# Attention and a mixture of experts on one core: small VectorE work moved or put in closed form, inputs loaded earlier, transfers issued a piece later

## The chip, the cores and the metric

The kernel runs on one core of one Trainium2 chip. The metric is the device time of one execution in microseconds. Five engines work from five queues of their own: TensorE (PE; the loading of its weights is shown apart as PEld), VectorE (DVE), ScalarE (ACT), GpSimd (POOL) and SyncE (SP), which here only issues transfers. [...]

## The reference

```python
# x: 8 sequences of 1024 tokens, 256 wide; 16 heads of 16; keys and values are one projection
x = x + attention(layernorm(x))          # softmax(q k^T / 4) k, then Wout and bout
y = layernorm(x)
x = x + moe(y)

def moe(x):                              # 8192 tokens
    scores = softmax(x @ gate_w.T)       # 8 experts
    vals, idx = top_k(scores.T, 1024)    # each expert takes its 1024 best tokens
    z = layernorm(x[idx]) * ln_w + ln_b
    out = gelu(z @ fc1.T + b1) @ fc2.T + b2
    return x.at[idx].add(out * vals)     # its own residual is inside
```

Every token passes three normalisations: before the attention (called a in the code), before the experts (b), and the expert's own (c), which normalises what b has already normalised.

## The kernel before

The first part is the attention with all that belongs to a token: projections, rotation, softmax, output projection, the second norm, the router. It runs over 8 batches (sequences) of 4 groups of heads; a group has 4 heads and takes 16 steps. A step handles one block of 128 keys for 512 queries (a half): scores for four heads, their exponentials, and in every second step the products with the values (`weigh_values`, L472). Step `s` counts from -15 to 512, so a batch has 64 steps, and batch b begins at step 64b.

The softmax needs the maximum of each query first. Row maxima are computed 15 steps ahead (`LEAD`): four matmuls in each step (L374), and after each a reduction of 512 scores on VectorE (L381). After each half of a group `lay_max` joins the two halves of the keys (L389), splits the result into a high and a low part (L391, L392), transposes both on TensorE (L398), and sends them through memory into `top_bufs` (L406, L410). They are added to the scores by a matmul eight steps after the half's last maximum.

The order on every engine is what the program writes; nothing is reordered. Beside the steps run three lists of tasks, written as generators: `urgent` (`lay_max`, and `divide`, which ends a half of a group), `starts` (the `prologue` of a later batch) and `ends` (the `epilogue` of each half of an earlier batch). A task says at each `yield` what it waits for: a number is a number of steps, "s" is at once, "y" needs a light step, "x" a heavy slot, of which each odd step has one. `run_pieces` (L622) goes through urgent, starts and ends in this order after each step, and of starts and ends it runs only the first task. A heavy slot goes to starts before ends.

The prologue of a batch loads x in two halves (L259), normalises them (L164 to L175), transposes (L184), projects (L303), rotates on GpSimd (L203 to L210), and splits queries, keys and the differences of keys (called steps) into high and low parts (`split_halves`, `split_steps`). `write_halves` (L216) writes these to memory, where `load_keys`, `load_steps` and `load_queries` fetch them for each group; `ready` and `steps_ready` say what has been written. High and low parts have two buffers each.

The epilogue fetches the residual (`residual`, L524) and adds the bias (L527), transposes and projects the attention's output (L548), adds (L556), takes the statistics for b (L164, L165, then two small GpSimd instructions L167, L169), scales the rows on GpSimd (`scaled`, L175), writes x plus y to the output (L562), takes statistics again for c and scales into `rows`, transposes (L184), and computes the router: a matmul (L579), a transpose (L590), and a small softmax (L593 to L605). In the last batch the scaling runs on VectorE. The value accumulators are added on GpSimd (L487).

Two places in the loop can run a task to its end at once. One is the start of a batch:

```python
if s > 0 and g == 0 and step == 0:
    while ends and ends[0].batch < b - 1:
        finish([ends[0]])
        ends.pop(0)
```

`finish` advances the task without a regard for slots, and the step's own matmuls come behind it. The other finishes the prologue when the keys or steps of a group are not there yet.

The second part finds each expert's tokens by 30 rounds of counting (L779 on), then gathers, computes and scatters (L860 on). The change does not touch it.

Of the kernel before, what the change touches and what calls it, by code (L numbers as in the profile page):

```python
# [18 lines left out]
P = 128  # L19
# [7 lines left out]
def preln_attention_moe_kernel(  # L27
# [50 lines left out]
    with ExitStack() as actx:  # L78
# [92 lines left out]

        def scaled(eng, dst, src, stats):
            mv, rstd = stats
            for t in range(T2):
                eng.tensor_scalar(  # L175
                    dst[:, t, :], src[:, t, :], mv[:, t, 0:1], rstd[:, t : t + 1],
                    ALU.subtract, ALU.mult,
                )
# [32 lines left out]

        def write_halves(d, rows, cols, hi, lo, keys):

            for part, src_t in enumerate((hi, lo)):
                pair = slice(part, None, 2) if keys else slice(2 * part, 2 * part + 2)
                nc.sync.dma_start(  # L216
                    d[rows, pair, cols], src_t.bitcast(F32).unsqueeze(1).to_broadcast([P, 2, QW])
                )

        def split_halves(b, hf, c, s, pt):  # L220

            q_d, k_d, _ = halves[b]
            first = b == 0 and c == 0
            hi = side.tile([P, QW], F32R, tag="hi", name="hi")
            lo = side.tile([P, QW], F32R, tag="lo", name="lo")
            full = None
            if first:
                nc.scalar.copy(hi, pt)
                nc.vector.tensor_tensor(lo, pt, hi.bitcast(F32), ALU.subtract)
            if not first or s == 1:  # L230
                full = side.tile([P, QW], F32, tag="full", name="full")
                nc.scalar.copy(full, pt)
            if not first:
                nc.gpsimd.tensor_copy(hi, full)
                nc.gpsimd.tensor_tensor(lo, full, hi.bitcast(F32), ALU.subtract)
            rows = slice(c * P, (c + 1) * P)
            if s == 0:
                write_halves(q_d[hf], rows, slice(0, QW), hi, lo, False)
            else:
                write_halves(k_d, rows, slice(hf * QW, (hf + 1) * QW), hi, lo, True)  # L240
            return full

        def split_steps(b, hf, c, full):


            dif = side.tile([P, QW], F32, tag="u", name="dif")
            nc.gpsimd.tensor_copy(dif[:, 0:P], full[:, 0:P])
            nc.gpsimd.tensor_tensor(dif[:, P:QW], full[:, P:QW], full[:, 0 : QW - P], ALU.subtract)
            hi = side.tile([P, QW], F32R, tag="hi", name="dhi")
            lo = side.tile([P, QW], F32R, tag="lo", name="dlo")  # L250
            nc.gpsimd.tensor_copy(hi, dif)
            nc.gpsimd.tensor_tensor(lo, dif, hi.bitcast(F32), ALU.subtract)
            write_halves(
                halves[b][2], slice(c * P, (c + 1) * P), slice(hf * QW, (hf + 1) * QW), hi, lo, True
            )
# [8 lines left out]
        def prologue(b):  # L264
# [7 lines left out]
            else:  # L272
                xts = [load_x(b, hf) for hf in range(2)]
                yield 2
# [36 lines left out]
            for c in range(DC):  # L311
                fulls = []
                for hf in range(2):
                    for s in range(2):
                        yield "x"
                        pt = transposed(lambda j: qks[hf][:, j, s, c * P : (c + 1) * P])
                        full = split_halves(b, hf, c, s, pt)
                    if hf == 1:
                        ready[(b, c)] = True
                    if b > 0 or c > 0:  # L320
                        yield 2
                        split_steps(b, hf, c, full)
                        yield 2
# [5 lines left out]
                steps_ready[(b, c)] = True  # L329
# [55 lines left out]
        def lay_max(i, hf):  # L385
# [3 lines left out]
            nc.vector.tensor_tensor(both, nm[:, 0], nm[:, 1], ALU.min)  # L389
            parts = small.tile([P, 4, 2, T2], F32R, tag="parts", name="parts")  # L390
            nc.vector.tensor_copy(parts[:, :, 0, :], both)  # L391
            nc.vector.tensor_tensor(  # L392
                parts[:, :, 1, :], both, parts[:, :, 0, :].bitcast(F32), ALU.subtract
            )
            yield 2
            yield "y"
# [7 lines left out]
            nc.scalar.copy(rows, pt[0 : 8 * T2, 0:P])  # L404
            top_d = dram.tile([2, 2, 2, QW], F32, tag="top_d", name="top_d", bufs=2)
            nc.sync.dma_start(  # L406
                top_d.rearrange("a h s (t q) -> (a h s t) q", q=P), rows
            )
            for h in range(2):
# [108 lines left out]
        def residual(b, hf):  # L518

            if (b, hf) not in residuals:  # L520
# [6 lines left out]
                nc.gpsimd.tensor_tensor(xt, xt, bo.unsqueeze(1).to_broadcast([P, T2, D]), ALU.add)  # L527
                residuals[(b, hf)] = xt
            return residuals[(b, hf)]

        def epilogue(b, hf):
# [4 lines left out]
            xt = residual(b, hf)  # L536
            yield "x"
# [23 lines left out]
            nc.gpsimd.tensor_tensor(xt, xt, xf, ALU.add)  # L561
            nc.sync.dma_start(out[b, tok, :].rearrange("(t p) d -> p t d", p=P), xt)  # L562
            yield 2

            rows = side.tile([P, T2, ROW], F32, tag="rows", name=f"rows_{b}_{hf}")
            if not last:
                stats = yield from row_stats(xf, "c")
                scaled(eng, rows[:, :, 0:D], xf, stats)
# [39 lines left out]
            if last:  # L608
                stats = yield from row_stats(xf, "c")
                scaled(eng, rows[:, :, 0:D], xf, stats)  # L610
# [56 lines left out]
        for s in range(-LEAD, n_steps + 1):  # L667
# [6 lines left out]
            if with_max and mstep == 0 and mi not in grp or with_exp and "steps" not in grp[i]:  # L674
                finish(starts)
                run_loads(s)
            if s == 0 or s > 0 and g == NG - 1 and step == T:
# [29 lines left out]
            if s == n_steps - 16:  # L707
                for hf in range(2):
                    residual(B - 1, hf)
# [318 lines left out]
```

## Time and profile before

| | |
|---|---|
| median of 3 runs | 2466.57 us (2464.75 to 2474.08) |
| profiled execution, its own time | 2478.25 us |
| its span, first to last instruction | 2476.5 us |
| score loop with its lead, about | 55 to 1800 us |
| TensorE busy | 87% |
| VectorE busy | 70% of the span; 85% from 500 to 1700 us |
| ScalarE, GpSimd busy | 55%, 51% |
| mean granted TensorE clock | 0.936 |

The profile is of one execution. Busy time counts an engine's instructions and not the waiting between them. In a row of a group, the two numbers after the bar are the time in which the group was busy and the mean length of one instruction in nanoseconds; the next is the time that the engine stood idle just before them, with what ended most of it. In the timeline, a row begins with the start and the length in microseconds, and a bracket gives the idle time before it and who ended it. PEclk is the clock that TensorE was granted, in tenths. A wait put down to one engine can have been for another, where the engine named was long done.

### The profile page before, as it was taken

How to read it: one execution, taken by the hardware profiler on the slowest of the kernel's cores; microseconds unless marked ns; L12 is line 12 of the kernel's file. 1: busy time of each engine (PE TensorE's matmuls, PEld its weight loads, DVE VectorE, ACT ScalarE, POOL GpSimd, SP SyncE). 2: the span in 40 equal slices, each digit the busy share in tenths (PEclk: the TensorE clock that was granted, in tenths of full speed). 3: DMA queues.
4: the chain of work that ended last, by engine and by line, in shares of the span. 5: the costliest groups of instructions: out<-in, count | busy, mean ns of one | idle time of the engine just before them, and what ended most of it. 6: DMA issues, size and time to landing. Idle time of an engine off the chain costs nothing. (4 is left out here: it accounts for less than half of the span.)

```text
span 2476.5 us, 34944 instructions
## 1 busy us (share of the span) xinstructions
PE 2149.9 (87%) x12692; PEld 1141.8 (46%) x12692; DVE 1740.0 (70%) x3303; ACT 1361.8 (55%) x1725; POOL 1253.4 (51%) x1188
## 2 busy tenths in 40 slices
PE   4999999988989989998998898999842189999998
PEld 2444444444544444444444344444321156666665
DVE  4988888887888888888888788999446833331111
ACT  1378777766777767776777676777820011111111
POOL 3365475648467665665674576544220144443332
PEclk7699999999999999999999999999965589999999
DMA  5514613532561453254235325331030023333322
GB/s 174 209 53 155 223 61 117 210 104 73 197 204 62 155 178 98 104 181 155 87 129 206 104 78 180 138 120 63 28 120 0 3 50 71 69 71 72 81 39 28
DMA packets 153564, 275.44 MB, mean 111 GB/s; under 512 B 14640, under 2 KB 66736, under 8 KB 153264
## 3 DMA queue, kind: packets, MB, share of 16 engines
q1 hardware_dynamic: 139984, 254.56, 29.7%
q0 software_dynamic: 12288, 17.05, 4.1%
q8 instruction: 100, 1.64, 0.3%
q10 hardware_dynamic: 1120, 1.61, 0.2%
q14 instruction: 72, 0.59, 0.1%
HBM read 146.02 MB, written 127.14 MB: 110 GB/s over the span
## 5 line engine op out<-in xcount | busy, mean ns | idle before, releaser
L381 DVE TENSOR_REDUCE nm<-ps_x 128x1 f32<-128x512 f32 x2048 | 1263.7, 681 | 211.7 <-PE ps_x L374 209.2
L453 ACT ACTIVATE e<-ps_s 128x1024 f32<-128x1024 f32 x1024 | 999.7, 1025 | 132.0 <-PE ps_x L374 77.0
L374 PE MATMUL ps_x<-k,q 64*128 64x512 f32 x2048 | 753.4, 460 | 41.3 <-DMA q<-q_d 17.3
L420 PE MATMUL ps_s<-q,s 64*128 64x512 f32 x2048 | 640.7, 430 | 9.3 <-ACT e L453 8.2
L374 PEld LDWEIGHTS ps_x<-k,q 64*128 64x128 f32 x2048 | 359.7, 190 | 450.7 <-DVE nm L381 295.1
L472 PE MATMUL ps_av<-e,v 128*32 128x512 f32 x4096 | 508.9, 616 | 42.6 <-DVE nm L381 39.2
L487 POOL TENSOR_TENSOR av<-av,avp 128x512 f32<-128x512 f32 x191 | 243.6, 1275 | 407.9 <-ACT avp L485 402.0
L420 PEld LDWEIGHTS ps_s<-q,s 64*128 64x128 f32 x2048 | 319.2, 187 | 42.6 <-ACT e L453 25.4
L939 ACT ACTIVATE hT<-ps_h,b 128x512 f32<-128x512 f32 x128 | 87.8, 687 | 369.5 <-PE ps_h L932 364.4
L954 DVE TENSOR_TENSOR o<-ps_o,b2b 128x256 f32<-128x256 f32 x64 | 27.2, 425 | 357.0 <-PE ps_o L946 357.0
L956 POOL DMA_INDIRECT out<-o,idx x64 | 127.2, 1988 | 281.8 <-DMA out<-o,idx 132.2
L472 PEld LDWEIGHTS ps_av<-e,v 128*32 128x32 f32 x4096 | 109.1, 111 | 292.8 <-issue 167.9
L932 PE MATMUL ps_h<-yT,w 128*128 128x512 f32 x512 | 225.8, 599 | 7.4 <-DVE yT L920 7.3
L946 PE MATMUL ps_o<-w,hT 128*128 128x256 f32 x1024 | 223.6, 379 | 0.0
L485 ACT COPY avp<-ps_av 128x512 f32<-128x512 f32 x192 | 112.6, 587 | 190.6 <-PE ps_av L472 179.4
L946 PEld LDWEIGHTS ps_o<-w,hT 128*128 128x128 f32 x1024 | 194.6, 190 | 33.3 <-issue 7.7
L420 PE MATMUL ps_s<-top,ones_r 64*128 64x512 f32 x512 | 151.7, 400 | 10.8 <-DMA top<-top_d 10.8
L932 PEld LDWEIGHTS ps_h<-yT,w 128*128 128x128 f32 x512 | 96.7, 191 | 125.0 <-issue 109.1
L904 POOL DMA_INDIRECT g<-rows_d,idx x64 | 70.5, 1102 | 147.4 <-DVE ids L879 128.2
L303 PE MATMUL ps_p<-wqkv,xnT 128*128 128x512 f32 x256 | 130.1, 636 | 15.4 <-DVE nm L381 15.0
L203 POOL TENSOR_TENSOR u<-pe,sin 128x256 f32<-128x256 f32 x112 | 79.1, 727 | 60.7 <-ACT pe L197 60.7
L420 PEld LDWEIGHTS ps_s<-top,ones_r 64*128 64x128 f32 x512 | 89.4, 189 | 20.6 <-DMA top<-top_d 12.1
(141 smaller groups left out, 1986.8 us busy)
## 6 DMA issues: line engine op xcount, KB each, us to landing
k<-k_d SPq DMA_DIRECT2D x64, 512.0 KB
q<-q_d SPq DMA_DIRECT2D x128, 256.0 KB
s<-s_d SPq DMA_DIRECT2D x64, 512.0 KB
q_d<-hi SPq DMA_DIRECT2D x32, 512.0 KB
q_d<-lo SPq DMA_DIRECT2D x32, 512.0 KB
k_d<-hi SPq DMA_DIRECT2D x32, 512.0 KB
k_d<-lo SPq DMA_DIRECT2D x32, 512.0 KB
s_d<-dhi SPq DMA_DIRECT2D x32, 512.0 KB
```

Of the source, the lines that this page charges most:

```text
L303: nc.tensor.matmul(pp, lhsT=xnT[:, c, j * P : (j + 1) * P], rhs=wqkv[:, c].rearrange("p a d -> p (a d)"), start=(c == 0), stop=(c == DC - 1),)
L374: nc.tensor.matmul(pt, lhsT=q[r : r + 64, h // 2, j * P : (j + 1) * P], rhs=k[r : r + 64, h // 2, kh * QW : (kh + 1) * QW], start=True, st ...
L381: nc.vector.tensor_reduce(grp[i]["nm"][:, kh, h, j : j + 1], pt, AX.X, ALU.max, negate=True)
L420: nc.tensor.matmul(pt[:, h % 2, :], lhsT=ones_r[r : r + 64, :] if last else k[r : r + 64, pair, kt * P : (kt + 1) * P], rhs=(top_bufs[half ...
L453: nc.scalar.activation(e.rearrange("p h q -> p (h q)"), pt.rearrange("p h q -> p (h q)"), AF.Exp, scale=DH**-0.5,)
L472: nc.tensor.matmul(pa[HS * h : HS * (h + 1), :], lhsT=v_bufs[b % 2][:, kt, c : c + HS], rhs=es[h // 2][:, h % 2, :], start=(n == 0), stop= ...
L485: nc.scalar.copy(part, pa)
L487: (nc.vector if end else nc.gpsimd).tensor_tensor(av, av, part, ALU.add)
L932: nc.tensor.matmul(ph, lhsT=w1[:, c, f * P : (f + 1) * P], rhs=yT[:, c, :], start=(c == 0), stop=(c == DC - 1),)
L939: nc.scalar.activation(hT[:, f, :], ph, AF.Gelu_apprx_tanh, bias=b1[:, e * FC + f : e * FC + f + 1])
L946: nc.tensor.matmul(po, lhsT=hT[:, f, j * P : (j + 1) * P], rhs=w2[:, f, :], start=(f == 0), stop=(f == FC - 1),)
L956: nc.gpsimd.indirect_dma_start(out=out_rows[:, :], out_offset=bass.IndirectOffsetOnAxis(ap=idx[:, t : t + 1], axis=0), in_=o, in_offset=No ...
```

## The change

It has six parts.

1. In `lay_max` the two halves are joined by one reduction instead of a minimum of two tensors; the high part is copied by ScalarE a step later, the low part subtracted by GpSimd another step later, the transpose comes a step after that, and the two transfers come one and three steps after it.
2. The statistics for c are not taken from the rows. Their variance follows from b's: `again` forms it in three small GpSimd instructions and a power, and the rows are scaled by one multiplication (their mean is nought). With it goes `row_stats` for c, in the last batch too.
3. The residual's bias becomes a step of its own, six steps after the load; in the last batch the bias comes six steps after the load too.
4. Inputs are loaded by a prologue that begins at step 48 of a batch instead of 56, and six steps pass before they are used, not two.
5. `write_halves` is put into a list, `pending`, and issued at the beginning of the prologue's next piece; `ready` and `steps_ready` are set there. The waits of two steps after `split_steps` are gone.
6. The output is written three steps after its sum is formed, not in the same step. The loop advances the prologue only until the group's keys or steps are there.

```diff
+        def again(stats):
+            mv, rstd = stats
+            var = small.tile([P, T2], F32, tag="ve_c", name="ve_c")
+            nc.gpsimd.tensor_tensor(var, rstd, rstd, ALU.mult)
+            nc.gpsimd.tensor_tensor(var, var, mv[:, :, 1], ALU.mult)
+            nc.gpsimd.tensor_scalar(var, var, EPS, None, ALU.add)
+            rstd2 = small.tile([P, T2], F32, tag="rs_c", name="rs_c")
+            nc.gpsimd.tensor_tensor(rstd2, var, mhalf[:, 0:T2], ALU.pow)
+            return rstd2
...
+        pending = []
+        def issue_pending():
+            while pending:
+                fn, *args = pending.pop(0)
+                fn(*args)
...
             if s == 0:
-                write_halves(q_d[hf], rows, slice(0, QW), hi, lo, False)
+                pending.append((write_halves, q_d[hf], rows, slice(0, QW), hi, lo, False))
...
-                yield 2
+                yield 6
             qks = []
...
                         yield "x"
+                        issue_pending()
                         pt = transposed(lambda j: qks[hf][:, j, s, c * P : (c + 1) * P])
                         full = split_halves(b, hf, c, s, pt)
...
                     if b > 0 or c > 0:
                         yield 2
+                        issue_pending()
                         split_steps(b, hf, c, full)
-                        yield 2
...
-            nc.vector.tensor_tensor(both, nm[:, 0], nm[:, 1], ALU.min)
+            nc.vector.tensor_reduce(both, nm.rearrange("p k h t -> p h t k"), AX.X, ALU.min)
             parts = small.tile([P, 4, 2, T2], F32R, tag="parts", name="parts")
-            nc.vector.tensor_copy(parts[:, :, 0, :], both)
-            nc.vector.tensor_tensor(
+            yield 1
+            nc.scalar.copy(parts[:, :, 0, :], both)
+            yield 1
+            nc.gpsimd.tensor_tensor(
                 parts[:, :, 1, :], both, parts[:, :, 0, :].bitcast(F32), ALU.subtract
             )
-            yield 2
-            yield "y"
+            yield 1
...
             nc.scalar.copy(rows, pt[0 : 8 * T2, 0:P])
+            yield 1
             top_d = dram.tile([2, 2, 2, QW], F32, tag="top_d", name="top_d", bufs=2)
...
+            yield 2
             for h in range(2):
...
             xt = residual(b, hf)
+            if not last:
+                yield 6
+                add_bias(xt)
             yield "x"
...
             nc.gpsimd.tensor_tensor(xt, xt, xf, ALU.add)
+            yield 3
             nc.sync.dma_start(out[b, tok, :].rearrange("(t p) d -> p t d", p=P), xt)
-            yield 2
...
+            rstd2 = again(stats)
+            def rows_scaled():
+                for t in range(T2):
+                    eng.tensor_scalar(
+                        rows[:, t, 0:D], xf[:, t, :], rstd2[:, t : t + 1], None, ALU.mult
+                    )
             if not last:
-                stats = yield from row_stats(xf, "c")
-                scaled(eng, rows[:, :, 0:D], xf, stats)
+                rows_scaled()
...
-            if with_max and mstep == 0 and mi not in grp or with_exp and "steps" not in grp[i]:
-                finish(starts)
+            while with_max and mi not in grp or with_exp and "steps" not in grp[i]:
+                starts[0].advance(s)
+                if starts[0].kind is None:
+                    starts.pop(0)
                 run_loads(s)
-            if s == 0 or s > 0 and g == NG - 1 and step == T:
+            if s == 0 or s > 0 and g == NG - 1 and step == 0:
...
-            if s == n_steps - 16:
+            if s in (n_steps - 16, n_steps - 10):
                 for hf in range(2):
-                    residual(B - 1, hf)
+                    xt = residual(B - 1, hf)
+                    if s == n_steps - 10:
+                        add_bias(xt)
```

More of the change, by code (lines that the diff above doesn't have):

```diff
@@ L237, in split_halves @@
             if s == 0:
-                write_halves(q_d[hf], rows, slice(0, QW), hi, lo, False)
+                pending.append((write_halves, q_d[hf], rows, slice(0, QW), hi, lo, False))
             else:
-                write_halves(k_d, rows, slice(hf * QW, (hf + 1) * QW), hi, lo, True)
+                cols = slice(hf * QW, (hf + 1) * QW)
+                pending.append((write_halves, k_d, rows, cols, hi, lo, True))
+                if hf == 1:
+                    pending.append((ready.setdefault, (b, c), True))
             return full
@@ L252, in split_steps @@
             nc.gpsimd.tensor_tensor(lo, dif, hi.bitcast(F32), ALU.subtract)
-            write_halves(
-                halves[b][2], slice(c * P, (c + 1) * P), slice(hf * QW, (hf + 1) * QW), hi, lo, True
-            )
+            rows, cols = slice(c * P, (c + 1) * P), slice(hf * QW, (hf + 1) * QW)
+            pending.append((write_halves, halves[b][2], rows, cols, hi, lo, True))
+            if hf == 1:
+                pending.append((steps_ready.setdefault, (b, c), True))
         def load_x(b, hf):
@@ L315, in prologue @@
                         yield "x"
+                        issue_pending()
                         pt = transposed(lambda j: qks[hf][:, j, s, c * P : (c + 1) * P])
                         full = split_halves(b, hf, c, s, pt)
-                    if hf == 1:
-                        ready[(b, c)] = True
+                        if b == 0 and c == 0:
+                            issue_pending()
                     if b > 0 or c > 0:
                         yield 2
+                        issue_pending()
                         split_steps(b, hf, c, full)
-                        yield 2
                     fulls.append(full)
@@ L328, in prologue @@
                         split_steps(b, hf, c, fulls[hf])
-                steps_ready[(b, c)] = True
+                        issue_pending()
+            yield 2
+            issue_pending()
         def load_keys(i):
@@ L408, in lay_max @@
             )
+            yield 2
             for h in range(2):
@@ L526, in residual, with add_bias @@
                 )
-                nc.gpsimd.tensor_tensor(xt, xt, bo.unsqueeze(1).to_broadcast([P, T2, D]), ALU.add)
                 residuals[(b, hf)] = xt
             return residuals[(b, hf)]
+        def add_bias(xt):
+            nc.gpsimd.tensor_tensor(xt, xt, bo.unsqueeze(1).to_broadcast([P, T2, D]), ALU.add)
         def epilogue(b, hf):
@@ L608, in epilogue @@
             if last:
-                stats = yield from row_stats(xf, "c")
-                scaled(eng, rows[:, :, 0:D], xf, stats)
+                rows_scaled()
             nc.sync.dma_start(
```

## The prediction

> **What bounds the kernel now.** I read the page first (engines, slices of the span), then the groups by line, the waits, and stretches of the timeline.
>
> ```profile
> PE 2149.9 (87%) x12692; PEld 1141.8 (46%) x12692; DVE 1740.0 (70%) x3303; ACT 1361.8 (55%) x1725; POOL 1253.4 (51%) x1188
> ...
> PEclk7699999999999999999999999999965589999999
> ```
>
> PEclk 9 says that TensorE has nearly its full clock in the loop, so a halved clock after a stop has something to take. Then the groups:
>
> ```profile
> L381 DVE TENSOR_REDUCE nm<-ps_x 128x1 f32<-128x512 f32 x2048 | 1263.7, 681 | 211.7 <-PE ps_x L374 209.2
> ...
> L392 DVE TENSOR_TENSOR parts<-both,parts 128x16 fp32r<-128x16 f32 x64 | 28.1, 440 | 2.2
> ...
> L389 DVE TENSOR_TENSOR both<-nm 128x16 f32<-128x16 f32 x64 | 21.3, 333 | 2.2
> ...
> L391 DVE CAST parts<-both 128x16 fp32r<-128x16 f32 x64 | 16.2, 253 | 2.2
> ```
>
> The score loop runs from about 93 to 1800 us, and TensorE and VectorE take turns in it: VectorE's 211.7 us of idle time before its maxima is nearly all a wait for scores. The timeline shows how:
>
> ```profile
> 608.88 2.48 DVE L381 TENSOR_REDUCE nm<-ps_x 128x1 f32<-128x512 f32 x4 [0.71 <-PE ps_x L374]
> ...
> 609.63 1.92 PE L472 MATMUL ps_av<-e,v 128*32 128x512 f32 x16
> ...
> 612.02 1.29 DVE L381 TENSOR_REDUCE nm<-ps_x 128x1 f32<-128x512 f32 x2 [0.65 <-PE ps_x L374]
> ```
>
> Four reductions take 2.48 us; in every second step TensorE spends 1.92 us on the values, VectorE runs dry, and about 0.66 us is lost. Two steps last 6.7 us on average (1667 us from step 0 to 496, over 248 pairs). Neither engine bounds alone: work added on one is partly hidden in the other's wait. But every engine runs in a written order, so a late answer stops TensorE. Such stops show as long pairs, and VectorE or SP can be behind them:
>
> ```profile
> 327.78 0.50 PE L374 MATMUL ps_x<-k,q 64*128 64x512 f32 x1 [2.16 <-DVE nm L381]
> ...
> 331.22 3.64 PE L472 MATMUL ps_av<-e,v 128*32 128x512 f32 x16 [0.86 <-DVE nm L381]
> ```
>
> ```profile
> 510.61 2.40 POOL L527 TENSOR_TENSOR xr<-xr,bo 128x1024 f32<-128x1024 f32 x1 [4.35 <-DMA xr<-in_x]
> ...
> 510.80 2.25 DVE L392 TENSOR_TENSOR parts<-both,parts 128x16 fp32r<-128x16 f32 x1
> ```
>
> The small subtraction of 16 numbers lasts 2.25 us, to the end of the GpSimd instruction beside it. SP's part: at 1378.40 VectorE has waited 5.98 us for an input whose load was issued only at 1371.95.
>
> **What the change takes away.**
>
> Maxima. Three VectorE instructions (333 + 253 + 440 = 1026 ns) become one reduction; nearest row: the router's reductions of 32 elements, about 180 ns. This work stands right after an even step's maxima, so it falls into the 0.66 us hole: 1.03 - 0.66 = 0.37 us stuck out, now nothing does. 64 x 0.37 = 24 us. The bounds are 0 and the whole 64 x 0.85 = 54 us.
>
> Second norm. 56 statistics (405 + 182 ns) leave VectorE in the loop, 33 us in all. The other statistics are in the same loop, and pairs with them are hardly longer than pairs without; I take 4 us, between 0 and 33.
>
> Long pairs (from the first maximum matmul of one even step to that of the next, less 6.7 us). With VectorE blocked or crowded by the removed work: 505.2 to 516.7, 650.1 to 660.2, 1058.5 to 1067.6, 327.8 to 338.9, 1145.9 to 1156.4: 4.8 + 3.4 + 2.4 + 4.4 + 3.8 = 18.8. TensorE waiting for the maxima's round trip, because SP stood before a key load whose source was just being written: 920.4 to 931.7, 1302.0 to 1314.9, 1527.4 to 1540.6: 17.3; there the new order puts two more steps between that write and that load, or its successors behind it. The late input at 1371.3 to 1387.7: 9.7; the input is now loaded 8 steps earlier, and six steps instead of two are left to it. Sum 46; bounds 20 and 55.
>
> End of the loop. The last half's second statistics, 1835.17 to 1838.86, go (3.7 us, and 0.8 for the half before, which overlaps TensorE): 4.5 us.
>
> Together 24 + 4 + 46 + 4.5 = 78.5 us.
>
> **What it adds.**
>
> First, drained batch starts. At step 64b the loop runs what is left of the batch before last's epilogue to its end, before the step's own matmuls. In the recorded order of the kernel before, that is at most one transpose and the softmax of the router (steps 320, 384, 448). The new waits (6 steps after the residual, 3 before the output, none given back by much) push it over: at steps 192 and 448 the row scaling has only just been queued, at 256, 320 and 384 the statistics too (256 even a projection), at 128 the router alone. Nothing covers this chain: TensorE stands until the transposes and router are through. Its price by rows: VectorE still has 1.5 us of maxima; four statistics 2.35 (two at 192 and 448: 1.17); then
>
> ```profile
> 1812.93 2.21 PE L184 MATMUL ps_t<-ident,xf 128*128 128x128 f32 x8 [4.90 <-DVE xf L175]
> ...
> 1816.85 0.48 PE L590 MATMUL ps_gt<-ident,lg 128*128 128x128 f32 x1 [0.39 <-ACT lg L587]
> ```
>
> 1.63 us from the last statistics to POOL's scaling (1360.99 to 1362.62), 4.84 for the scaling, and from its end to the router's last transpose 3.6 us (1813.75 to 1817.33 at the loop's end, the one place where the trace shows this chain undiluted; the lines above are its TensorE part). Less 2.2 us of matmuls that were needed anyway: 11.7 us three times, 10.5 twice, 0.8 for the projection, 1.8 at 128: 59 us. Lower bound 40, if the scaling's first tiles release TensorE early.
>
> Second, TensorE behind GpSimd. The low half of the maxima is now computed on POOL (no row of this shape; its smallest take 233 ns, its 384-wide subtraction 1006; I take 350), and one step later TensorE's transpose waits for it. POOL's queue is in order. A rotation is 4.4 us (2 x 0.73 + 1.28 + 1.28 + 0.40), a normalised input 6.2, the first norm with its residual 8.6, the second norm rows plus the four small instructions 6.7. The rows' scaling now has one operation instead of two: between 0.6 and 1.22 us each. From the end of step 77 to the transpose of step 83 POOL must do rotation, first norm, rotation, input, second norm, rotation, two additions of 1.27: 35 to 38 us, where six steps last 22: TensorE stands about 15. At steps 203, 267, 331 and 395 three or four rotations, an input and the bias (2.4) leave about 4 each, at 235 4.7, five others 3 in all: 39 us. Bounds 10 (real steps there are longer, POOL keeps up) and 60 (buffers of hi and lo wait for transfers now issued a piece later). ScalarE's 64 small copies (about 0.24 each, in its idle time) 2 us. The maxima's transfers now end two steps before their use instead of four; at steps 46 and 166 they come behind a key load that waits for its source: 5 us for both.
>
> Third, the clock. After the 2.16 us wait above the values took 3.64 us instead of 1.92. The three waits for maxima (2.47, 3.78, 4.55 us) made their pairs 4.6, 6.2 and 6.5 longer: some 2 us more than the wait. "TensorE: Matmul & The Clock Gate" of the Trainium skill (Part 1, the clock gate) says that one idle window of about 3.4 us halves the rate and that a busy window restores it, which speaks against any change that gathers stops. By the rule one or two half-rate windows cost 1.7 to 3.4 us a stop, 19 to 37 us for eleven stops (83, five starts, 203, 267, 331, 395, 235); by the rows 22. I take the rows.
>
> Sum: 59 + 39 + 7 + 22 = 127 lost, 78.5 won: +48.5. The profiled execution took 2478.25 us (span 2476.5 and 1.75 around it): 2526.7. It lies 11.7 above the median of the runs, 2466.57, so 2515.
>
> **Rivals.** (a) POOL keeps pace and starts drain faster: 40 for the starts, 10 for POOL, 7 and 12 (six stops), 69 against 78.5: -10, so 2457, within 12 us of no change. For it: POOL is idle half of the span; against it: the one wait of TensorE for POOL today (2.79 us at 589.42) comes in just such a row of rotations and scaling. (b) Faster: VectorE sets the pace, place the maxima's reductions, price the 54 + 33 us taken from it. If they come off whole, the gain is 87 + 46 + 4.5 = 137.5 against 127 (2456), and against 108 with the starts at 40 it is 2437. It turns the sign from 88% of the freed time upward (127 - 50.5 = 76.5 of 87), with the cheaper starts from 66%. Against it: 211.7 us of idle time that VectorE has now. (c) Much slower: hi and lo have two buffers; their transfer is issued two steps later, and 1 MB took some 8 us to land (issued to 1292.2, the load behind it at 1299.8). POOL then waits in each of the 84 pieces of batches 1 to 7, two thirds of a microsecond or so: +56, 2571. (d) That the changed kernel does not do what it says: the order of instructions shows that it does; 0.
>
> **Numbers.** Forecast 0.62, (a) 0.14, (b) 0.13, (c) 0.11. The forecast's own range is 2480 to 2550. To hold 8 in 10 the range reaches down to 2450, into (a) and part of (b), and up to 2560, short of (c). A measurement of this kernel tells about 0.5%, 12 us, from no change. Faster takes (b) and a little: 0.14; same most of (a): 0.13; slower the forecast and (c): 0.73.
>
> **What would show it.** Right: TensorE waits of 8 us or more at the starts of batches 3 to 7, a wait of over 10 in step 83 with POOL named, half-rate clock after each; the statistics of xf gone, the new reduction near 0.18 us, no VectorE row of 2 us beside POOL; no wait of 5 us for x. Wrong: batch starts under 4 us, or POOL's low half never late; then (a) or (b).

## The result, and the profile after

The changed kernel takes 2559.03 us, the median of 4 runs (2557.93 to 2561.76); the kernel before took 2468.61 us beside it (4 runs). The ratio is 1.0366, with a 95% interval of 1.0343 to 1.0389: 90 us slower, where the forecast was 2515. That is outside the forecast's own range (2480 to 2550) and just inside the wide one (2450 to 2560). The profiled execution's span is 2560.0 us.

The page of the changed kernel, engines and granted clock:

```profile
PE 2174.6 (85%) x12692; PEld 1159.3 (45%) x12692; DVE 1660.9 (65%) x3047; ACT 1372.4 (54%) x1789; POOL 1254.3 (49%) x1284
...
PEclk7799989999989998999899899989985579999999
```

VectorE has been relieved as planned, from 1740.0 to 1660.9 us, and the execution is longer. The clock row was a solid row of nines in the loop; now an 8 stands in it at regular distances. TensorE stops there.

The groups by line, each shape by itself (busy time, mean ns of one, idle time before it with what ended most of it):

```profile
L408 DVE TENSOR_REDUCE nm<-ps_x 128x1 f32<-128x512 f32 x2048 | 1265.4, 682 | 335.3 <-PE ps_x L401 334.2
...
L187 POOL TENSOR_SCALAR xf<-xr,mv_b,rs_b 128x256 f32<-128x256 f32 x56 | 67.9, 1225 | 1.5
L605 POOL TENSOR_SCALAR rows<-xf,rs_c 128x256 f32<-128x256 f32 x56 | 50.9, 926 | 1.5
L164 DVE BATCH_NORM_STATS2 bnst<-x 128x6 f32<-128x256 f32 x64 | 26.0, 406 | 0.0
...
L421 POOL TENSOR_TENSOR parts<-both,parts 128x16 fp32r<-128x16 f32 x64 | 14.3, 224 | 25.0 <-ACT parts L419 25.0
L419 ACT CAST parts<-both 128x16 fp32r<-128x16 f32 x64 | 13.1, 205 | 0.0
L416 DVE TENSOR_REDUCE both<-nm 128x16 f32<-128x32 f32 x64 | 12.0, 188 | 7.1
```

The maxima's reductions (L408) take what they took, but VectorE now waits 334.2 us for scores where it waited 209.2. Most of the difference is not the time taken from VectorE: in experiment 1, without the stops behind GpSimd, the wait is 226.6 us. The wait of 6.0 us for an input (L164) is gone.

What TensorE waits for (total us, times, longest), first one row of the kernel before, then the changed kernel:

```profile
PE ps_s L420 <- DMA top<-top_d: 10.8, 3, 4.6
```

```profile
PE ps_l L426 <- POOL parts L421: 98.4, 29, 19.1
PE ps_t L196 <- POOL xf L187: 39.9, 20, 5.9
...
PE ps_s L450 <- DMA top<-top_d: 3.5, 3, 1.4
```

The first row of the changed kernel did not exist before: it is the transpose of the maxima waiting for GpSimd's low half. The second is the row scaling in drained batch starts. The third shows the maxima's transfers, which the kernel before had waited for 10.8 us, all but off the path.

One of the stops of the first row, GpSimd's timeline (start, length), and TensorE's in the same stretch:

```profile
1019.79 0.23 POOL L167 TENSOR_SCALAR ve_a<-mv_a 128x4 f32<-128x4 f32 x1
1020.10 1.04 POOL L169 TENSOR_TENSOR rs_a<-ve_a,mhalf 128x4 f32<-128x4 f32 x1
1021.25 4.85 POOL L187 TENSOR_SCALAR x<-x,mv_a,rs_a 128x256 f32<-128x256 f32 x4
1026.07 1.27 POOL L517 TENSOR_TENSOR av<-av,avp 128x512 f32<-128x512 f32 x1
1027.29 2.39 POOL L561 TENSOR_TENSOR xr<-xr,bo 128x1024 f32<-128x1024 f32 x1
...
1034.18 1.26 POOL L517 TENSOR_TENSOR av<-av,avp 128x512 f32<-128x512 f32 x1
...
1039.54 0.40 POOL L222 COPY v<-qk 128x256 f32<-128x256 f32 x1
1039.90 0.23 POOL L421 TENSOR_TENSOR parts<-both,parts 128x16 fp32r<-128x16 f32 x1
```

```profile
1040.18 0.40 PE L426 MATMUL ps_l<-ident,parts 128*32 128x128 f32 x1 [8.09 <-POOL parts L421]
```

GpSimd works without a gap for 20 us (most of the rows left out belong to two rotations); the instruction of 0.23 us that TensorE needs is the last of the row, and TensorE has stood since 1032.1. This is step 267; the same 8.1 us stop comes in steps 203, 331 and 395, because batches repeat.

A drained batch start, VectorE, GpSimd and TensorE of the changed kernel at step 256:

```profile
980.58 0.42 DVE L164 BATCH_NORM_STATS2 bnst<-xr 128x6 f32<-128x256 f32 x1
...
984.35 4.85 POOL L187 TENSOR_SCALAR xf<-xr,mv_b,rs_b 128x256 f32<-128x256 f32 x4
985.63 0.18 PEld L196 LDWEIGHTS ps_t<-ident,xf 128*128 128x128 f32 x1 [6.10 <-POOL xf L187]
...
992.29 0.47 PE L632 MATMUL ps_gt<-ident,lg 128*128 128x128 f32 x1 [0.39 <-ACT lg L629]
...
992.70 0.79 PE L401 MATMUL ps_x<-k,q 64*128 64x512 f32 x1
```

The chain is the forecast's: projection until about 980, statistics, scaling, transposes, router, and only at 992.70 the step's own scores. Between 980 and 992 TensorE is busy for 3.99 of 12 us.

Where the 83.5 us between the two spans came from, measured as in the prediction (a pair is two steps, from the first maximum matmul of an even step to that of the next; "longer" means above 6.7 us; the means leave out the last pair):

| | before | after |
|---|---|---|
| loop, step 0 to 496 | 1667.5 | 1751.3 |
| lead, step -15 to 0 | 38.0 | 41.6 |
| behind step 496 | 716.2 | 714.7 |
| mean of the pairs up to 8.3 us | 6.495 | 6.403 |
| pairs over 8.3 us: number, sum of what is longer | 12, 55 | 23, 158 |
| of these, drained starts (pairs 126, 190, 254, 318, 382, 446) | | 63 |

The ordinary pair became 0.09 us faster, some 21 us in all. The long pairs of before are gone, and nearly three times their sum came in their place.

### The profile page after: what moved, and what is told of

It is laid out like the page before. It is cut to its first block, busy times and chain, and to the rows that moved or that the text cites. A ratio compares the mean times of both kernels' runs of the same rounds, so it can differ in the third digit from the quotient of the medians.

```text
span 2560.0 us, 34891 instructions
## 1 busy us (share of the span) xinstructions
PE 2174.6 (85%) x12692; PEld 1159.3 (45%) x12692; DVE 1660.9 (65%) x3047; ACT 1372.4 (54%) x1789; POOL 1254.3 (49%) x1284
## 5 line engine op out<-in xcount | busy, mean ns | idle before, releaser
L408 DVE TENSOR_REDUCE nm<-ps_x 128x1 f32<-128x512 f32 x2048 | 1265.4, 682 | 335.3 <-PE ps_x L401 334.2
L450 PE MATMUL ps_s<-q,s 64*128 64x512 f32 x2048 | 647.6, 436 | 10.9 <-ACT e L483 7.8
L401 PEld LDWEIGHTS ps_x<-k,q 64*128 64x128 f32 x2048 | 366.6, 192 | 431.4 <-DVE nm L408 288.2
L502 PE MATMUL ps_av<-e,v 128*32 128x512 f32 x4096 | 502.6, 609 | 20.1 <-DVE nm L408 15.1
L517 POOL TENSOR_TENSOR av<-av,avp 128x512 f32<-128x512 f32 x191 | 243.2, 1273 | 515.2 <-ACT avp L515 515.1
L450 PE MATMUL ps_s<-top,ones_r 64*128 64x512 f32 x512 | 163.1, 422 | 3.5 <-DMA top<-top_d 3.5
L426 PE MATMUL ps_l<-ident,parts 128*32 128x128 f32 x64 | 19.0, 297 | 102.1 <-POOL parts L421 98.4
```

The lines of the kernel that those rows point to most:

```text
L401: nc.tensor.matmul(pt, lhsT=q[r : r + 64, h // 2, j * P : (j + 1) * P], rhs=k[r : r + 64, h // 2, kh * QW : (kh + 1) * QW], start=True, st ...
L408: nc.vector.tensor_reduce(grp[i]["nm"][:, kh, h, j : j + 1], pt, AX.X, ALU.max, negate=True)
L450: nc.tensor.matmul(pt[:, h % 2, :], lhsT=ones_r[r : r + 64, :] if last else k[r : r + 64, pair, kt * P : (kt + 1) * P], rhs=(top_bufs[half ...
L502: nc.tensor.matmul(pa[HS * h : HS * (h + 1), :], lhsT=v_bufs[b % 2][:, kt, c : c + HS], rhs=es[h // 2][:, h % 2, :], start=(n == 0), stop= ...
L517: (nc.vector if end else nc.gpsimd).tensor_tensor(av, av, part, ALU.add)
```

## The experiments

All ratios compare medians with the kernel before on the same chip. Two experiments compared with each other ran in part on different chips; where their ratios give another difference than their medians, both are given. "Parts" is the tile with the high and low halves of the maxima, "top" the tile into which their transfers bring them.

**1. The low half on VectorE.** The changed kernel, with one word of it undone.

```diff
-            nc.gpsimd.tensor_tensor(
+            nc.vector.tensor_tensor(
                 parts[:, :, 1, :], both, parts[:, :, 0, :].bitcast(F32), ALU.subtract
```

> The changed kernel with one edit: the low half of the maxima is subtracted on VectorE in the same step instead of on GpSimd. Theory (TensorE's transpose waits for this subtraction because it stands behind rotations and scalings in GpSimd's queue): the changed kernel's TensorE waits for it 98 us, with the halved clock after each some 20 to 30 more; these go, and the low half costs VectorE 64 x 0.44 us at most: 2559 falls by 75 to 105, to about 2465. Rival (the maxima come late for another reason, ScalarE's copy or the transfers behind it, or TensorE waits elsewhere as long once it stops waiting here): at most 25 us are won, 2535 or more. The drained batch starts, five waits for the scaling on GpSimd of 5.7 to 5.9 us, should stand unchanged.

Measured: 2467.18 us, ratio 0.9989 (0.9979 to 1.0000). The waits of its TensorE:

```profile
PE ps_t L196 <- POOL xf L187: 39.8, 20, 5.9
...
PE ps_l L426 <- DVE nm L408: 4.6, 7, 0.9
```

The row of 98.4 us is gone, and 91.9 us of time with it; the drained starts' pairs have the lengths they had (17.6, 20.9, 19.2, 19.2, 17.6). So GpSimd's queue in front of one small instruction accounts for as much as the whole loss.

**2. The epilogue's waits undone.** The changed kernel without the six steps before the bias, and with the output written at once.

```diff
             if not last:
-                yield 6
                 add_bias(xt)
...
-            yield 3
             nc.sync.dma_start(out[b, tok, :].rearrange("(t p) d -> p t d", p=P), xt)
+            yield 2
```

> The changed kernel with the epilogue's waits as they were: bias in the step of the residual's load, output written in the step of its sum and two steps after it. In the written order nothing of an epilogue is then left at a batch's start. Theory (drained batch starts cost 63 us: pairs of steps 126, 190, 254, 318, 382, 446 are 2.4, 10.9, 14.2, 12.5, 12.5 and 10.9 us over 6.7): 2559 falls by 45 to 65, to about 2503; GpSimd waits for the residual again (65.7 us before) and may delay the low half more, which could take 10 to 20 of it back. Rival (the drain only gathers in one place what costs as much spread out): 15 us or less are won, 2545 or more.

Measured: 2560.78 us, ratio 1.0370 (1.0344 to 1.0396), as long as the changed kernel itself. The waits of its TensorE:

```profile
PE ps_l L426 <- POOL parts L421: 79.4, 27, 8.1
PE ps_s L450 <- DMA top<-top_d: 56.5, 11, 7.6
```

The row scaling is gone from the list, so the starts drain no more. In its place is a wait for the maxima's transfers, 56.5 us of it. The theory forecast 45 to 65 us less, the rival 15 or less; nothing was won, but not for the rival's reason, as experiment 5 shows: one edit had removed one wait and made another.

**3. Both.** Experiments 1 and 2 in one kernel.

> The changed kernel with both edits: low half on VectorE, epilogue's waits as they were. Theory: the two costs add, 2559 - 90 - 55, about 2410 to 2425, under the kernel before (2468), since what the change takes from VectorE and SP's queue is worth some 50 us or more. Rival (the gain counted from long pairs and from VectorE's holes isn't there): 2455 or more, no faster than before.

Measured: 2490.34 us, ratio 1.0088 (1.0058 to 1.0119): a miss. The waits of its TensorE, then SP's timeline and TensorE's in one of them:

```profile
PE ps_s L450 <- DMA top<-top_d: 66.1, 16, 7.6
```

```profile
528.28 0.33 SPq L435 DMA_DIRECT2D top_d<-mrows  x1
546.35 0.39 SPq L596 DMA_DIRECT2D out<-xr  x1
546.84 0.71 SPq L440 DMA_DIRECT2D top<-top_d  x2
```

```profile
549.85 0.79 PE L450 MATMUL ps_s<-top,ones_r 64*128 64x512 f32 x2 [7.47 <-DMA top<-top_d]
```

SP stands before the output's write, which waits for GpSimd's sum (that ended at 546.33). The second transfers of the maxima are queued behind it, though the first transfer, which writes what they fetch, was issued at 528.28, and TensorE waits 7.47 us for them. Where the write comes three steps after the sum, this is rarer but not gone: with the output's timing as the only difference, experiment 5 below waits 14.6 us for the transfers instead of 66.1. The change's later transfers are nearly harmless only together with its later output.

**4. The closed form alone.** The kernel before with `again` and `rows_scaled`, nothing else.

```diff
+            rstd2 = again(stats)
...
-                stats = yield from row_stats(xf, "c")
-                scaled(eng, rows[:, :, 0:D], xf, stats)
+                rows_scaled()
```

> The kernel before with the second norm's closed form alone. It takes 64 statistics (0.405 + 0.182 us) from VectorE, 33 us in the loop and 4.5 at its end, and spares two pieces of each epilogue. Theory (VectorE's small work is mostly hidden in its holes): 5 to 20 us faster than before, about 2455. Rival (VectorE sets the pace): 35 us or more, 2432 or less.

Measured: 2447.01 us, ratio 0.9919 (0.9889 to 0.9948), 24 us less rather than 5 to 20. Ordinary pairs went from 6.495 to 6.461 us, which is 8 us in all; the sum of what long pairs are longer fell from 55 to 34; the rest behind step 496 fell by 3.8. These add up to 34 us, as between the two profiled executions; the medians say 24, because the profiled execution of the kernel before, 2478.25 us, lies above its median. Its VectorE rows:

```profile
L164 DVE BATCH_NORM_STATS2 bnst<-x 128x6 f32<-128x256 f32 x64 | 26.0, 406 | 0.0
L164 DVE BATCH_NORM_STATS2 bnst<-xr 128x6 f32<-128x256 f32 x64 | 25.9, 405 | 0.0
```

The statistics of xf are gone, and so is the wait for an input, although this kernel loads its inputs no earlier than the kernel before.

**5. No wait before the bias.** Experiment 1 without the six steps; the output keeps its three.

```diff
             if not last:
-                yield 6
                 add_bias(xt)
```

> The changed kernel with the low half on VectorE, and the bias added in the step of the residual's load; the output keeps its three steps. In the written order no epilogue is then left at a batch's start. In the run with all of the epilogue's old waits the drains were gone too, but TensorE waited 66 us for the maxima's transfers instead. Theory (those waits came from the output's write, which SP held until GpSimd had its sum, with the maxima behind it; the drains do cost 50 to 63 us): here neither is there, and 2467 falls by 40 to 60, to about 2415. Rival (the drains cost nothing of their own, the work fills the time elsewhere): 2455 or more.

Measured: 2414.64 us, ratio 0.9773 (0.9745 to 0.9802). Against experiment 1 that is 52.5 us, what is won by not draining the starts. The waits of TensorE for row scaling (39.8 us) are gone, and of the transfers' waits more are left than in experiment 1 (8.4):

```profile
PE ps_s L450 <- DMA top<-top_d: 14.6, 5, 3.9
```

**6. The second transfer a step sooner.** Experiment 5, with the step between the two transfers of the maxima shortened.

```diff
                 top_d.rearrange("a h s (t q) -> (a h s t) q", q=P), rows
             )
-            yield 2
+            yield 1
```

> As e5_no_bias_wait, and the second of the maxima's transfers is written one step after the first, not two, ahead of a prologue's writes in SP's queue. Theory (the change left these transfers no slack, so each thing before them in SP's queue is waited for): the remaining short waits of TensorE for them, 1.2 to 1.6 us five or six times with the low half on VectorE, go: 5 to 12 us faster than e5_no_bias_wait. Rival (they land in time in e5_no_bias_wait already, or the key loads before them decide): within 4 us of it.

Measured: 2400.24 us, ratio 0.9704 (0.9678 to 0.9731). This beats both kernels: 2.96% below the one before, and 159 us below the changed one. The same row:

```profile
PE ps_s L450 <- DMA top<-top_d: 3.7, 3, 2.1
```

10.9 us of waiting less gave 14.4 us of time (17 by the ratios).

**7. The new joining of the maxima alone.** The kernel before with the changed `lay_max`.

```diff
-            nc.vector.tensor_tensor(both, nm[:, 0], nm[:, 1], ALU.min)
+            nc.vector.tensor_reduce(both, nm.rearrange("p k h t -> p h t k"), AX.X, ALU.min)
             parts = small.tile([P, 4, 2, T2], F32R, tag="parts", name="parts")
-            nc.vector.tensor_copy(parts[:, :, 0, :], both)
-            nc.vector.tensor_tensor(
+            yield 1
+            nc.scalar.copy(parts[:, :, 0, :], both)
+            yield 1
+            nc.gpsimd.tensor_tensor(
...
-            yield 2
-            yield "y"
+            yield 1
```

with the steps before and between the transfers as well.

> The kernel before with the new joining of the maxima alone (one reduction, high part on ScalarE, low part on GpSimd, transfers later). Theory (the low half waits in GpSimd's queue in any version): TensorE waits for it, and this part alone is slower than before, by 20 to 80 us, about 2515. Rival (the GpSimd queue is only too long through the new epilogue and its second norm): TensorE waits under 15 us for it, and this part alone is 5 to 20 us faster than before.

Measured: 2608.17 us, ratio 1.0554 (1.0529 to 1.0580), worse than either theory put it, and worse than the whole change. The waits of its TensorE:

```profile
PE ps_l L399 <- POOL parts L394: 101.5, 27, 14.0
PE ps_s L423 <- DMA top<-top_d: 44.4, 11, 5.7
```

Both waits at once: GpSimd's queue, and an output write in front of the later transfers.

**8. The same with the low half on VectorE.** Experiment 7 with the word of experiment 1.

> The kernel before with the same joining alone, but its low half on VectorE. Against e7_lay_max_alone it shows GpSimd's part. Theory: 24 us faster than before, less what the transfers lose by their later place in SP's queue, where outputs wait for GpSimd again: 2445 to 2475. Rival (later transfers decide): slower than 2490, with TensorE waiting 30 us or more for the maxima's transfers.

Measured: 2509.42 us, ratio 1.0157 (1.0134 to 1.0180). I had expected it to be below the kernel before; it is above, and the rival, that the later transfers decide, holds. Against experiment 7 GpSimd's part is 99 us. The wait left is the transfers':

```profile
PE ps_s L423 <- DMA top<-top_d: 56.7, 13, 7.5
```

**9. The old joining in the changed kernel.** The changed kernel with the whole `lay_max` of before: three VectorE instructions at once, all transfers at once.

```diff
-            nc.vector.tensor_reduce(both, nm.rearrange("p k h t -> p h t k"), AX.X, ALU.min)
+            nc.vector.tensor_tensor(both, nm[:, 0], nm[:, 1], ALU.min)
...
-            yield 1
-            nc.scalar.copy(parts[:, :, 0, :], both)
-            yield 1
-            nc.gpsimd.tensor_tensor(
+            nc.vector.tensor_copy(parts[:, :, 0, :], both)
+            nc.vector.tensor_tensor(
...
-            yield 1
+            yield 2
+            yield "y"
```

> The changed kernel with the whole of the earlier way of joining the maxima put back: three VectorE instructions at once (minimum, cast, subtraction), the transpose two steps later at a light step, all three transfers behind it at once. Everything else is as changed, so the drained batch starts stay. To be compared with the kernel in which only the low half went to VectorE (2467 us). Theory, from the prediction's first term: the three small instructions right after an even step's maxima stick out of VectorE's idle stretch, 24 us in all, so about 2490 (2480 to 2500). Rival: the staging of the join brings nothing, since TensorE's waits for VectorE end in the same place; then 2455 to 2470, and TensorE's waits for the maxima's transfers stay under 5 us in sum.

Measured: 2476.31 us, ratio 1.0022 (1.0013 to 1.0030), between the two theories. It is 9 us above experiment 1, while its TensorE waits 0.7 us for the transfers instead of 8.4: by this sum the crowded VectorE costs some 17 us, and the sooner transfers give 8 of it back.

**10. The old timing without the drained starts.** Experiment 5 with reduction, cast and subtraction on VectorE at once and all transfers at once.

```diff
-            yield 1
-            nc.scalar.copy(parts[:, :, 0, :], both)
-            yield 1
+            nc.vector.tensor_copy(parts[:, :, 0, :], both)
...
-            yield 1
+            yield 2
+            yield "y"
```

> The kernel without the bias wait and with the low half on VectorE (2414.6 us), its join of the maxima by one reduction, cast and subtraction on VectorE at once, the transpose two steps later at a light step, all three transfers at once. So two VectorE instructions of about 0.25 and 0.44 us crowd in right after the maxima of 64 even steps, and the transfers leave as early as in the kernel before. Theory: the transfers' earlier start takes off most of the 14.6 us that TensorE waited for them (about 10), the crowding costs up to 64 x 0.3 = 19: 2415 to 2430, slower than the one with the second transfer one step sooner (2400). Rival: crowding costs nothing, 2395 to 2405.

Measured: 2414.40 us, ratio 0.9762 (0.9744 to 0.9779): as long as experiment 5, at the edge of the theory's range, 14 us above experiment 6. TensorE no longer waits for the transfers at all. Between the profiled executions the loop is 17.9 us longer than in experiment 6, and 17.7 of it lies in the 62 pairs whose first step has the join (one pair in four), so it is VectorE's two instructions in the wrong place. But it is not spread evenly: 35 of the 62 pairs differ by less than 0.1 us, and eight by more than 1 us. The two instructions (minimum, median and maximum ns) show why:

```profile
L418 DVE CAST parts<-both x64: 174/175/2392, 74.4 to 1707.8; 128x16 fp32r<-128x16 f32 x64
L419 DVE TENSOR_TENSOR parts<-both,parts x64: 174/176/1206, 74.6 to 1708.0; 128x16 fp32r<-128x16 f32 x64
```

At its median length the join, 188 + 175 + 176 ns = 0.54 us, fits into the idle time of 0.66 us that the prediction found; what sticks out is the few long ones. The prediction's working with mean lengths (0.19 + 0.25 + 0.44 - 0.66 = 0.22 us, 64 times) also gives 14 us, but by luck.

**11. Inputs loaded late again.** Experiment 6, its prologue beginning at step 56 of a batch and waiting two steps.

```diff
-            if s == 0 or s > 0 and g == NG - 1 and step == 0:
+            if s == 0 or s > 0 and g == NG - 1 and step == T:
...
-                yield 6
+                yield 2
```

> The best version so far (low half on VectorE, no wait before the bias, second transfer a step sooner; 2400 us), with the inputs loaded as in the kernel before: the prologue begins at step 56 of a batch, and two steps pass before the inputs are used. Theory, from the prediction's long pairs: the late input comes back, about 10 us in one or more batches, 2408 to 2430, and a wait of VectorE for x of 5 us or more stands in the list. Rival: the late input of the kernel before was a matter of what stood in SP's queue in that one batch (the closed form alone lost it too), so nothing returns: 2395 to 2405, and no such wait.

Measured: 2405.65 us, ratio 0.9748 (0.9732 to 0.9765), a little above experiment 6, at the edge of the rival's range. No wait of VectorE for x stands in its list. So the earlier loads are worth 5 us by the medians and 11 by the ratios, whose intervals just fail to overlap, but not by way of a late input.

**12. Halves written at once.** Experiment 6, where an entry put into `pending` is executed immediately.

```diff
-        pending = []
+        class Now(list):
+            def append(self, item):
+                item[0](*item[1:])
+
+        pending = Now()
```

> The best version so far (2400 us), with the high and low parts of queries, keys and steps written at once as in the kernel before, not a piece later. Theory, from the prediction's long pairs: SP stands again before writes whose low part GpSimd has not finished, with key loads and the maxima's transfers behind them, which made TensorE wait in three pairs of the kernel before, 17 us in all: 2412 to 2425, and the waits for top rise from 3.7 to 10 us or more. Rival: the transfers have enough slack now and nothing returns: 2395 to 2405.

Measured: 2420.42 us, ratio 0.9806 (0.9789 to 0.9822), 20 us above experiment 6 (25 by the ratios), as the theory had it. The waits of TensorE, and SP's own (lines stand four further down here):

```profile
PE ps_s L454 <- DMA top<-top_d: 21.3, 6, 7.9
```

```profile
SPq L240 <- POOL hi L258: 214.9, 43, 14.9
```

SP's wait in front of these writes was 217.9 us in the kernel before, 111.0 in the changed one and 98.2 in experiment 6. The two longest pairs, 360 and 424 (14.8 and 15.7 us), begin at the steps at which the kernel before had two of its three waits for the maxima; the third, at 248, does not come back. In the main the staged writes do what the prediction said of them.

## Why the prediction was right in direction and short by half

Each step of its sum with what was measured:

| step | forecast | measured | by |
|---|---|---|---|
| maxima and second norm in ordinary pairs | -28 | about -21 | 6.495 to 6.403 us, 225 to 235 pairs |
| of it, maxima | -24 | -14 to -17 | experiments 10 and 9 |
| of it, second norm | -4 | -8 | ordinary pairs of experiment 4 |
| long pairs | -46 | about -47 | 55 before, 8.5 left in experiment 1 outside of batch starts |
| end of the loop | -4.5 | -1.5; -4.2 in experiment 1 | behind step 496 |
| drained starts, with their clock | 59 + 10 | 63 in the trace, 52.5 by the runs | pairs; experiments 1 and 5 |
| TensorE behind GpSimd, with its clock | 39 + 12 | 92 | experiment 1 |
| copies and transfers behind key loads | 7 | 3.5 in the changed kernel, 8.4 and 14.6 in experiments 1 and 5 | waits for top; the copies' part not measured |

**The gains** were sized well as a sum, -70 of -78.5, but in part by luck. The 24 us for the maxima were worked out from mean lengths of the three instructions; at their median length (176 + 175 + 176 ns) they fit into the idle time, and only the long ones stick out (experiment 10). And the long pairs had more than one cause each: experiment 4 removes 21 of their 55 us with the closed form alone, among them the pair of the late input (380), which the prediction had booked on the earlier load; experiment 11, with late loads, has no such wait either. The 17.3 us booked on the staged writes fit experiment 12 (20 us), though one of the three pairs did not return there.

**The step that failed** is the second of the losses, TensorE behind GpSimd: its place and its cause were right, its size was not. At step 83 it said about 15 us and the trace has 19.07. For steps 203, 267, 331 and 395 it said about 4 each, and it is 8.1: the list of GpSimd's work had rotations, an input and the bias, but not the additions of the value accumulators (L517). Two of these, 2.5 us, lie in the row shown above; the other 1.6 us of the difference stay open. At 235 it said 4.7, and it is 6.24. For five others, which it does not name, it said 3 us in all: the next five in size, steps 171, 251, 299, 363 and 427, took 17.7. Eighteen more, one in the lead of 4.5 us and most others of about 1 us, were not foreseen. It asked where GpSimd falls behind for several steps, and priced a small instruction at its own length (350 ns estimated, 224 measured); the true price is whatever stands before it in the queue, and in 29 of its 64 uses that kept TensorE waiting. The upper bound given, 60, was exceeded too.

**The drained starts** were right in place, chain and price. From experiment 1 to experiment 5 their six pairs become 69 us shorter, the 59 + 10 of the forecast. But the loop becomes only 51.5 us shorter, since the work then stands in other pairs, some 6 us of it as waits for the maxima's transfers, which rise from 8.4 to 14.6 us. That part the forecast did not see.

**The clock** was priced at 2 us a stop. Experiment 1 has nearly the same order without the stops behind GpSimd, so its pairs are the measure:

| step | stop, us | its pair and the next, longer than in experiment 1 |
|---|---|---|
| 83 | 19.07 | 19.8 |
| 203, 267, 331, 395 | 8.1 | 9.6, 9.3, 9.6, 9.2 |
| 235 | 6.24 | 8.3 |

So a stop costs 0.7 to 2.1 us beyond its own length, 1.35 on average: the forecast was right in kind and somewhat high. In the sum over all 29 stops nothing of it is left, 98.4 us of waiting against 96.8 us between the two spans; experiment 1 waits longer elsewhere (for the transfers 8.4 us instead of 3.5).

Stretches around the first, changed kernel (start:end, length, then busy time and pieces by engine, granted clock, DMA share):

```profile
358.00:378.00 20.00, 1.07 (x3) 0.56 (x4) 1.60 (x3) 1.60 (x3) 18.04 (x23) 0.59 0.19 74
378.00:392.00 14.00, 13.99 (x84) 6.70 (x82) 8.58 (x15) 8.76 (x12) 5.78 (x7) 0.85 0.01 2
392.00:400.00 8.00, 7.98 (x45) 3.65 (x44) 6.53 (x13) 6.42 (x8) 5.91 (x7) 1.00 0.23 69
```

The stop lasts from 357.86 to 376.93. Most of the low clock lies inside it, where it costs nothing. In the 14 us from 378, 0.85 is what half rate for the first 4.2 of them would give (14 x 0.15 / 0.5); with the 1.1 us from 376.93 to 378 that is 5.3 us at half rate once TensorE runs again, which takes 2.6 us from it. The rule of "TensorE: Matmul & The Clock Gate" (Part 1) that the prediction weighed, half rate until a window of about 3.4 us has been busy, agrees with that if the window in which the stop ended did not count. Of the 2.6 us the pair shows 1.2 (27.20 us against 6.95 in experiment 1); that VectorE's own work covers the rest is likely and not shown.

**The rivals.** (a), that GpSimd keeps pace, is excluded by 29 stops. (b), that VectorE sets the pace, priced the gain at 137.5 us. With both costs taken away the same change gains 69 us (experiment 6), and VectorE still waits 216.4 us for scores there. (c), that hi and lo wait for their transfers, would be a wait of GpSimd for a transfer. The largest such rows of the changed kernel are these:

```profile
POOL hi L254 <- DMA s_d<-dhi: 17.5, 2, 13.9
POOL dhi L274 <- DMA q_d<-hi: 14.0, 3, 7.7
```

With the small ones of lo they make 38.2 us in 14 waits, and the kernel before has 32.4 of the same kind: 6 us more, where (c) had 56. That the number of (c), 2571, was nearer than the forecast's is no argument for it.

**What the result hides.** The forecast treated the sum as gains against two costs. The runs show that the costs are not the change's idea but two places of it: with the low half on VectorE and the bias not delayed, the same change is 2.3% faster than the kernel before (experiment 5), and 3.0% with the second transfer a step sooner (experiment 6).

## What to carry to other kernels

A small instruction moved to a half-idle engine costs what stands before it in that engine's queue, if another engine waits for it in order; add up the longest run of work there between the producer and the consumer, every kind of instruction included, not the busy share. A wait put into a task that is later run to its end without regard for slots only moves the work to where nothing hides it. And undo edits in pairs: moving a transfer later was nearly harmless here only because another edit had moved a blocking write out of its way, and that one, undone alone, looked worthless (experiment 2).

## What the runs showed of the hardware

VectorE's small instructions are not of one length. The same tiles, kernel before and then changed kernel (minimum, median and maximum ns):

```profile
L391 DVE CAST parts<-both x64: 174/175/1204, 76.3 to 1764.7; 128x16 fp32r<-128x16 f32 x64
L392 DVE TENSOR_TENSOR parts<-both,parts x64: 174/176/2249, 76.5 to 1764.9; 128x16 fp32r<-128x16 f32 x64
```

```profile
L416 DVE TENSOR_REDUCE both<-nm x64: 186/188/192, 74.2 to 1849.6; 128x16 f32<-128x32 f32 x64
L421 POOL TENSOR_TENSOR parts<-both,parts x64: 216/223/235, 84.6 to 1852.4; 128x16 fp32r<-128x16 f32 x64
```

The subtraction's mean of 440 ns is a median of 176 with a tail up to 2249, and the prediction found that longest one ending with the GpSimd instruction beside it. The reduction of the same data with one input never took over 192 ns in 64, with GpSimd just as busy. "SBUF: two separate sides" in the Trainium skill's page "SBUF — State Buffer" has the rule behind it: VectorE shares a port pair with GpSimd as an exclusive lock, which its instruction needs in a two-port mode, or with two inputs from SBUF against a GpSimd instruction that reads there. The cast has one input and a tail as well (1204 ns, and 2392 in experiment 10). The same section names an fp32 copy within SBUF as one that runs in such a mode; that this cast does is likely, but no trace here shows it.

GpSimd's scaling of 256 numbers takes 1225 ns with two operations and 926 ns with one (L187, L605); an operation less saved a quarter.
